# Attention loop: the values' products a round later, six tiles of exponentials

## The chip, the cores and the metric

The kernel runs on one core of a Trainium2 chip. The metric is the device time of one execution in microseconds; the time of a kernel is the median of several runs. The engines are TensorE (PE, with its weight loads listed apart as PEld), VectorE (DVE), ScalarE (ACT), GpSimd (POOL) and SyncE (SP). Each works through its own instructions in the order in which the program has them, and waits for the others by semaphores.

## The reference

Two layers over an image batch of 4 x 64 x 64 x 128 numbers in float32. Layer 0 is a selective scan in three directions. Layer 1 is attention on tokens (16 heads of width 8, where query, key and value are the same vectors), followed by a small dense part, and by experts that pick 8 of 4096 tokens each. What the change touches is the middle of the attention:

```
q = jnp.transpose(qkv, (0, 2, 1, 3))                       # 4 images, 16 heads, 4096 tokens, 8
scores = jnp.einsum('bhsd,bhtd->bhst', q, q) / np.sqrt(D)
attn = jax.nn.softmax(scores, axis=-1)
ctx = jnp.einsum('bhst,bhtd->bhsd', attn, q)
```

## The kernel before, in words

**The attention loop.** `Attention.loop(b, beside)` does this for one image, and runs four times. The 16 heads are taken four at a time (`j`, with the heads 4k + j for k from 0 to 3), the 4096 queries in 8 blocks of 512 (`qb`), the 4096 keys in 32 blocks of 128 (`kc`). A round `i` is one (j, qb, kc), so an image has 4 x 8 x 32 = 1024 rounds and the kernel 4096. The text calls the score products of a round S and the value products V.

- `scores(i)` issues S: four matmuls (L833), one for each of the four heads, each on 32 rows of PE. Two heads share a score tile in PSUM of 2 x 512 columns (`s`, pool `a_ps_s`, three buffers). So a round has a first and a second pair, and two exponentials on ACT (L838), each from a score tile into a tile `e` in SBUF (pool `a_exps`, four buffers). No maximum is subtracted.
- `values(i)` issues V: four matmuls (L847), one for each head, each on 32 columns of PE, that add the exponentials' product with the values to `acc` (pool `a_ps_o`, one buffer). The values carry a column of ones, so that the softmax's denominators are summed along. The sum runs over the 32 rounds of one (j, qb).
- `sums(j, qb, i)` comes after the last of these 32 rounds: ACT copies `acc` to a tile `av` (L856), and the four stores of the heads' results (L862) and the one of the denominators (L865) are put on POOL's queue three rounds later, out of the dictionary `later`. There are 4 x 8 x 4 = 128 such copies.
- `masked(j, qb)` makes the block of queries `qm` in which all but the four heads are zero (DVE, L822), 12 rounds ahead.

The profile records two passes for each of these float32 matmuls, so a round shows eight records of S and eight of V.

**Order.** The loop runs under a manual schedule: each engine gets its instructions in the order in which the code issues them. Before the first round there is `scores(0)`; round i issues `scores(i + 1)`, then `values(i)`, then the copy if a sum has ended, then a mask and stores if they are due, then `beside(i)`. On PE that is S(1), V(0), work beside, S(2), V(1), work beside, and so on; on ACT the two exponentials of round i + 1, the copy, then the beside-work.

**Work beside.** `beside(i)` gives a step to generators that hold the next image's selective scan (exponentials on ACT at L495, scans on DVE at L507, sums over the states on PE at L515, copies of the scan's end values on POOL at L508, stores on POOL from L534 on) and the dense work of the images before and after. In the fourth loop there is no scan left, and little beside-work at all.

[...]

Of the kernel before, what the change touches and what calls it, by code (L numbers as in the profile page):

```python
# [11 lines left out]
F32 = mybir.dt.float32  # L12
# [4 lines left out]
P = 128  # L17
C = 128
L = 4096
NT = L // P  # L20
# [12 lines left out]
QB = 512  # L33
# [570 lines left out]
class Attention:  # L604

    def __init__(self, tc, ctx, loop, w, gate, cols, ident, bank, dram, t1, w_out, sums, sz, x):
        nc = self.nc = tc.nc
        gate_w, gate_b = gate  # L610
# [25 lines left out]
        with tc.tile_pool(name="a_load", bufs=1) as load, tc.tile_pool(  # L636
            name="a_load_ps", bufs=2, space=PSUM
# [36 lines left out]
        nc.gpsimd.memset(self.heads[:, :, :, D], 1.0)  # L674
        self.small = ctx.enter_context(tc.tile_pool(name="a_small", bufs=2))
        self.pieces_of(loop, 2)
        self.big = loop.enter_context(tc.tile_pool(name="a_big", bufs=1))
        self.mid = loop.enter_context(tc.tile_pool(name="a_mid", bufs=2))
        self.exps = loop.enter_context(tc.tile_pool(name="a_exps", bufs=4))
        self.ps_s = loop.enter_context(tc.tile_pool(name="a_ps_s", bufs=3, space=PSUM))  # L680
        self.ps_o = loop.enter_context(tc.tile_pool(name="a_ps_o", bufs=1, space=PSUM))
        self.u, self.q, self.v, self.context, self.total, self.t2 = {}, {}, {}, {}, {}, {}
# [123 lines left out]

    def loop(self, b, beside):

        nc = self.nc
        self.context[b] = self.dram.tile([P, L], F32, name=f"d_ctx_{b}")  # L810
        self.total[b] = self.dram.tile([H, L], F32, name=f"d_sum_{b}")
        qT = self.big.tile([P, L], F32, tag="qT", name=f"qT_{b}")
        v = self.big.tile([P, NT, VPAD], F32, tag="v", name=f"v_{b}")
        for g in range(NT // 4):
            nc.sync.dma_start(out=qT[:, g * 512 : (g + 1) * 512], in_=self.q[b][:, g * 512 : (g + 1) * 512])
            nc.sync.dma_start(out=v[:, g * 4 : g * 4 + 4, :], in_=self.v[b][:, g * 4 : g * 4 + 4, :])
        rounds = [(j, qb, kc) for j in range(4) for qb in range(L // QB) for kc in range(NT)]
        queries, es, accs, later = {}, {}, {}, {}

        def masked(j, qb):  # L820
            t = self.mid.tile([P, QB], F32, tag="qm", name=f"qm_{b}_{j}_{qb}")
            nc.vector.tensor_scalar_mul(t, qT[:, qb * QB : (qb + 1) * QB], self.mask[:, j : j + 1])  # L822
            queries[j, qb] = t

        def scores(i):

            j, qb, kc = rounds[i]
            es[i] = []
            for pair in range(2):
                s_ps = self.ps_s.tile([P, 2, QB], F32, tag="s", name=f"s_{b}_{i}_{pair}")  # L830
                for k in range(2):
                    at = 32 * (2 * pair + k)
                    nc.tensor.matmul(  # L833
                        s_ps[:, k, :], qT[at : at + 32, kc * P : (kc + 1) * P], queries[j, qb][at : at + 32, :],
                        start=True, stop=True,
                    )
                e = self.exps.tile([P, 2, QB], F32, tag="e", name=f"e_{b}_{i}_{pair}")
                nc.scalar.activation(e, s_ps, AF.Exp, scale=1.0 / math.sqrt(D))  # L838
                es[i].append(e)

        def values(i):
            j, qb, kc = rounds[i]
            if kc == 0:
                accs[j, qb] = self.ps_o.tile([P, QB], F32, tag="acc", name=f"acc_{b}_{j}_{qb}")
            for k in range(4):
                h = 4 * k + j
                nc.tensor.matmul(  # L847
                    accs[j, qb][32 * k : 32 * k + 32, :], v[:, kc, h * VW : h * VW + 32],
                    es[i][k // 2][:, k % 2, :], start=(kc == 0), stop=(kc == NT - 1),
                )  # L850
            del es[i]

        def sums(j, qb, i):

            av = self.mid.tile([P, QB], F32, tag="av", name=f"av_{b}_{j}_{qb}")
            nc.scalar.copy(av, accs.pop((j, qb)))  # L856
            cut = slice(qb * QB, (qb + 1) * QB)

            def store():
                for k in range(4):  # L860
                    h = 4 * k + j
                    nc.gpsimd.dma_start(  # L862
                        out=self.context[b][h * D : h * D + D, cut], in_=av[32 * k : 32 * k + D, :]
                    )
                nc.gpsimd.dma_start(  # L865
                    out=self.total[b].rearrange("(k j) t -> j k t", j=4)[j, :, cut], in_=av[D::32, :]
                )

            later[i + 3] = store

        masked(0, 0)
        scores(0)
        for i, (j, qb, kc) in enumerate(rounds):
            if i + 1 < len(rounds):
                scores(i + 1)
            values(i)
            if kc == NT - 1:
                sums(j, qb, i)
            if kc == NT - 12 and i + 12 < len(rounds):
                masked(*rounds[i + 12][:2])  # L880
            if i in later:
                later.pop(i)()
            beside(i)
        for i in sorted(later):
            later[i]()

# [389 lines left out]
def tile_kernel(tc, ctx, x, in_proj_w, dirs, out_proj_w, attn, gate, weight1, weight2, out):  # L1276
# [16 lines left out]
    with ExitStack() as fill:  # L1293
# [7 lines left out]
        with tc.manual_schedule():  # L1301
# [5 lines left out]
            others.rest()  # L1307
    loop = ExitStack()
    block = Attention(tc, ctx, loop, attn, gate, cols, ident, bank, dram, t1, w_out, scans.sums, inputs.sz, x)

    def opening(b):
# [91 lines left out]
```

## Time and profile before

Three runs took 13392.09, 13397.82 and 13401.96 us, the median is 13397.82. The profiled execution took 13404.59 us, the span from its first to its last instruction is 13402.9 us, and PE's mean granted clock was 0.943.

| stretch (us from the start) | what runs | us | per round | PE busy | ACT busy | DVE busy | granted clock |
|---|---|---|---|---|---|---|---|
| 2810.5 to 5371.6 | loop of image 0 | 2561.1 | 2.50 | 2536.7 | 2380.5 | 2091.4 | 0.99 |
| 5371.6 to 7999.5 | loop of image 1 | 2627.9 | 2.57 | 2566.2 | 2382.5 | 2149.1 | 0.99 |
| 7999.5 to 10590.1 | loop of image 2 | 2590.6 | 2.53 | 2544.6 | 2341.9 | 1954.4 | 0.99 |
| 10590.1 to 12952.6 | loop of image 3 | 2362.5 | 2.31 | 2351.8 | 2004.4 | 212.5 | 1.00 |

Busy times are those in which the engine has at least one instruction under way. Matmuls overlap, and the ends that the profile gives for them are modelled; so PE's busy share tells that it is rarely empty, not how fast it goes. For that one compares the starts of successive groups. The table's stretches begin where the first score product of an image starts; between them lie only some microseconds. Before 2810 us lie the inputs and the first image's scan, after 12953 us the last image's dense part and the experts.

For the copies and stores: the copy L856 takes 585 to 727 ns (median 593) and runs 128 times; the stores at L862 take 502 to 606 ns (median 520) to issue, 512 times, and land 1.7 to 8.7 us after that (median 2.2).

### The profile page before, as it was taken

Reading aid. Unit: us, or ns where it says so; the run is one execution under the profiler, and the core shown is the slowest. Engines: PE = TensorE matmul, PEld = TensorE weight load, DVE = VectorE, ACT = ScalarE, POOL = GpSimd, SP = SyncE. Lnnn points to the kernel's source line nnn. Section 1 sums busy time; section 2 is a strip of 40 time slices with the busy share of each in tenths; the row PEclk is TensorE's granted clock in tenths of the full one; section 3 lists DMA queues with packets and bytes.
Section 4 is the critical chain, followed back from the end, with each engine's and each line's share of the span. In section 5 each row is a group of like instructions: output and inputs, shape, how many; then the busy total and the mean of one; then the engine's idle time right before and its main releaser. Section 6 shows DMA issues by size and latency. Waiting matters only on the chain. (4 is left out here: it accounts for less than half of the span.)

```text
span 13402.9 us, 213892 instructions
## 1 busy us (share of the span) xinstructions
PE 12305.7 (92%) x85255; PEld 3948.9 (29%) x85255; DVE 8969.0 (67%) x8565; ACT 10704.2 (80%) x10807; POOL 3464.3 (26%) x4192
## 2 busy tenths in 40 slices
PE   7797978369999999999999999999999999999976
PEld 3232333112222222233332222333323222222224
DVE  6998989678888877888888679888884210000014
ACT  5665656269999998899999889999998888888851
POOL 2333334222333322223333223333331000000001
PEclk8887988679999999999999999999999999999986
DMA  5666666544444444544444545444443100000015
GB/s 143 185 181 178 193 176 194 154 121 120 117 120 113 107 127 120 142 112 116 111 112 112 130 126 130 107 115 114 110 113 98 51 19 9 9 7 30 12 36 178
DMA packets 703778, 1490.44 MB, mean 111 GB/s; under 512 B 185406, under 2 KB 318838, under 8 KB 702774
## 3 DMA queue, kind: packets, MB, share of 16 engines
q1 hardware_dynamic: 512078, 1057.83, 30.6%
q0 software_dynamic: 139584, 300.84, 7.2%
q10 hardware_dynamic: 51112, 118.08, 3.3%
q8 instruction: 667, 10.93, 0.3%
q14 instruction: 337, 2.76, 0.1%
HBM read 1167.22 MB, written 308.94 MB: 110 GB/s over the span
## 5 line engine op out<-in xcount | busy, mean ns | idle before, releaser
L838 ACT ACTIVATE e<-s 128x1024 f32<-128x1024 f32 x8192 | 7905.3, 1027 | 1026.3 <-PE s L833 847.4
L833 PE MATMUL s<-qm,qT 32*128 32x512 f32 x32768 | 5416.6, 642 | 127.9 <-DVE qm L822 76.3
L847 PE MATMUL acc<-e,v 128*32 128x512 f32 x32768 | 4387.5, 607 | 25.1 <-ACT av L856 22.1
L508 POOL COPY ends<-h 128x1 f32<-128x1 f32 x1536 | 1841.9, 1199 | 5104.7 <-DVE h L507 5088.8
L833 PEld LDWEIGHTS s<-qm,qT 32*128 32x128 f32 x32768 | 1790.0, 183 | 3288.8 <-PE s L833 1438.0
L847 PEld LDWEIGHTS acc<-e,v 128*32 128x32 f32 x32768 | 647.0, 108 | 3163.7 <-issue 3027.8
L507 DVE TENSOR_TENSOR_SCAN h<-dA,ends,dB 128x1024 f32<-128x1024 f32 x576 | 1374.5, 2386 | 197.9 <-ACT dA L495 140.9
L507 DVE TENSOR_TENSOR_SCAN h<-delta,ends,du 128x1024 f32<-128x1024 f32 x576 | 1354.1, 2351 | 164.7 <-ACT delta L495 95.5
L495 ACT ACTIVATE dA<-delta,A 128x1024 f32<-128x1024 f32 x768 | 886.8, 1155 | 339.6 <-DMA delta<-d_delta 217.7
L504 DVE TENSOR_TENSOR dB<-du,B 128x1024 f32<-128x1024 f32 x768 | 935.2, 1218 | 211.8 <-PE y L515 193.1
L495 ACT ACTIVATE delta<-delta,A 128x1024 f32<-128x1024 f32 x768 | 886.6, 1154 | 179.4 <-PE y L515 168.8
L509 DVE TENSOR_TENSOR du<-h,C 128x1024 f32<-128x1024 f32 x768 | 940.7, 1225 | 26.3
L509 DVE TENSOR_TENSOR dB<-h,C 128x1024 f32<-128x1024 f32 x768 | 940.7, 1225 | 26.3
L504 DVE TENSOR_TENSOR du<-du,B 128x1024 f32<-128x1024 f32 x768 | 934.2, 1216 | 0.0
L862 POOL DMA_DIRECT2D d_ctx<-av x512 | 262.2, 520 | 1615.9 <-ACT av L856 1609.4
L515 PE MATMUL y<-dB,sel 128*32 128x256 f32 x6144 | 498.1, 397 | 124.3 <-DVE o L531 109.3
L361 PE MATMUL cv<-xn,conv 128*128 128x512 f32 x1024 | 492.4, 640 | 40.7 <-DVE xn L298 18.4
L515 PE MATMUL y<-du,sel 128*32 128x256 f32 x6144 | 494.2, 395 | 25.3 <-DVE du L509 25.3
L507 DVE TENSOR_TENSOR_SCAN h<-dA,dB 128x1024 f32<-128x1024 f32 x192 | 446.9, 2328 | 54.1 <-ACT dA L495 32.1
L507 DVE TENSOR_TENSOR_SCAN h<-delta,du 128x1024 f32<-128x1024 f32 x192 | 440.1, 2292 | 43.1 <-ACT delta L495 18.7
L531 DVE SCALAR_TENSOR_TENSOR o<-us,D,y 128x256 f32<-128x256 f32 x384 | 206.1, 537 | 353.3 <-PE y L515 353.1
L414 PE MATMUL sp<-s,minus 128*128 128x512 f32 x384 | 222.4, 663 | 207.7 <-ACT s L408 207.7
(248 smaller groups left out, 7676.3 us busy)
## 6 DMA issues: line engine op xcount, KB each, us to landing
delta<-d_delta SPq DMA_DIRECT2D x768, 512.0 KB
du<-d_du SPq DMA_DIRECT2D x576, 512.0 KB
du<-d_du ACTq DMA_DIRECT2D x192, 512.0 KB
d_u<-u POOLq DMA_DIRECT2D x48, 1024.0 KB, 5.6
B<-d_bc SPq DMA_DIRECT2D x96, 512.0 KB
C<-d_bc SPq DMA_DIRECT2D x96, 512.0 KB
d_delta<-r POOLq DMA_DIRECT2D x48, 1024.0 KB, 5.4
d_du<-u POOLq DMA_DIRECT2D x48, 1024.0 KB, 6.6
```

The source lines that it names most:

```text
L361: nc.tensor.matmul(ps[:, cut], w["conv"][:, k, m * P : (m + 1) * P], reads(k, g), start=(k == 0), stop=(k == 3))
L414: nc.tensor.matmul(ps[:, cut], sign, t[:, m, cut], start=(i == 0), stop=(i == 2))
L495: nc.scalar.activation(tiles["delta", s], t, AF.Exp, scale=A)
L504: nc.vector.tensor_mul(dB, du, spread[order, c, "B", j % 2])
L507: nc.vector.tensor_tensor_scan(h, dA, dB, first, ALU.mult, ALU.add)
L508: nc.gpsimd.tensor_copy(ends[order, c][:, at : at + 1], h[:, T - 1 :])
L509: nc.vector.tensor_mul(dB, h, spread[order, c, "C", j % 2])
L515: nc.tensor.matmul(y[32 * g : 32 * g + 32, : T // 4], self.sel[:, j // 2, :], hC[:, 256 * g : 256 * g + 256], start=(j == 0), stop=(j == 3),)
L833: nc.tensor.matmul(s_ps[:, k, :], qT[at : at + 32, kc * P : (kc + 1) * P], queries[j, qb][at : at + 32, :], start=True, stop=True,)
L838: nc.scalar.activation(e, s_ps, AF.Exp, scale=1.0 / math.sqrt(D))
L847: nc.tensor.matmul(accs[j, qb][32 * k : 32 * k + 32, :], v[:, kc, h * VW : h * VW + 32], es[i][k // 2][:, k % 2, :], start=(kc == 0), stop ...
L862: nc.gpsimd.dma_start(out=self.context[b][h * D : h * D + D, cut], in_=av[32 * k : 32 * k + D, :])
```

## The change

V is issued a round later. Round i still begins with `scores(i + 1)`, and then issues `values(i - 1)`, not `values(i)`; the last V of an image follows after its last round. The copy and the stores of a finished sum are now called out of `values`, so they come a round later too, the stores still three rounds after their copy. The pool of exponentials grows from four tiles to six, and `av` goes from two tiles to one.

```diff
-        self.exps = loop.enter_context(tc.tile_pool(name="a_exps", bufs=4))
+        self.exps = loop.enter_context(tc.tile_pool(name="a_exps", bufs=6))
@@ values
             del es[i]
+            if kc == NT - 1:
+                sums(j, qb, i)
@@ sums
-            av = self.mid.tile([P, QB], F32, tag="av", name=f"av_{b}_{j}_{qb}")
+            av = self.mid.tile([P, QB], F32, tag="av", bufs=1, name=f"av_{b}_{j}_{qb}")
             nc.scalar.copy(av, accs.pop((j, qb)))
...
-            later[i + 3] = store
+            later[i + 4] = store
@@ the rounds
             if i + 1 < len(rounds):
                 scores(i + 1)
-            values(i)
-            if kc == NT - 1:
-                sums(j, qb, i)
+            if i:
+                values(i - 1)
             if kc == NT - 12 and i + 12 < len(rounds):
                 masked(*rounds[i + 12][:2])
             if i in later:
                 later.pop(i)()
             beside(i)
+        values(len(rounds) - 1)
         for i in sorted(later):
             later[i]()
```

An `e` tile has 2 x 512 float32 numbers in each partition, 4 KB; an `av` tile has 2 KB.

## The prediction

> **What bounds the kernel now.** First I read where the time lies: busy time by stretch puts the four attention loops at 2561, 2628, 2591 and 2363 us of a span of 13402.9, so 76% of it, with PE busy for 98 to 100% of each and ACT for 85 to 93%. The costliest groups on the page come next (busy us, mean ns, idle before and what ended it):
>
> ```profile
> L838 ACT ACTIVATE e<-s 128x1024 f32<-128x1024 f32 x8192 | 7905.3, 1027 | 1026.3 <-PE s L833 847.4
> L833 PE MATMUL s<-qm,qT 32*128 32x512 f32 x32768 | 5416.6, 642 | 127.9 <-DVE qm L822 76.3
> L847 PE MATMUL acc<-e,v 128*32 128x512 f32 x32768 | 4387.5, 607 | 25.1 <-ACT av L856 22.1
> ```
>
> There are 4096 rounds, so 8192 exponentials of 1.03 us, and in each round eight recorded matmuls of scores (S) and eight of values (V), which overlap. ACT waits for scores, 847 us; PE hardly waits for anything that these rows name. As a busy PE is not a PE at its peak, the timeline of a quiet stretch in the last loop, where only S, V and exponentials run, is the third view (start, length, engine, line, count, idle before):
>
> ```profile
> 11500.44 1.07 PE L847 MATMUL acc<-e,v 128*32 128x512 f32 x8
> 11500.60 4.01 ACT L838 ACTIVATE e<-s 128x1024 f32<-128x1024 f32 x4 [0.36 <-PE s L833]
> 11501.44 1.37 PE L833 MATMUL s<-qm,qT 32*128 32x512 f32 x8
> 11502.74 1.07 PE L847 MATMUL acc<-e,v 128*32 128x512 f32 x8
> 11503.73 1.14 PE L833 MATMUL s<-qm,qT 32*128 32x512 f32 x8
> 11504.81 1.07 PE L847 MATMUL acc<-e,v 128*32 128x512 f32 x8
> 11504.97 4.01 ACT L838 ACTIVATE e<-s 128x1024 f32<-128x1024 f32 x4 [0.36 <-PE s L833]
> 11505.80 1.37 PE L833 MATMUL s<-qm,qT 32*128 32x512 f32 x8
> 11507.10 1.07 PE L847 MATMUL acc<-e,v 128*32 128x512 f32 x8
> ```
>
> Starts tell more than lengths here. From V at 11500.44 to V at 11504.81 two rounds take 4.37 us: V 1.00, S 1.30, V 0.99, S 1.08. Without a wait a round would be 1.00 + 1.07 = 2.07, two of them 4.14, so 0.23 us are lost, all inside every second S. The exponentials tell why. The batch from 11504.97 ends its first one at about 11505.99 (1.02 us); S at 11505.80 has begun with its first pair of heads, and its second pair needs a score tile that this exponential reads (there are three score tiles, `a_ps_s`). It starts some 0.24 us late. So a circle sets the pace: first pair of S (1.13 us), exponential (1.02, with 0.15 for handing on), second pair of the next S, then V, then S again: 2.30 + 2.07 = 4.37 us for two rounds.
>
> And what does V wait for? Its last exponential belongs to the batch that ends at 11500.60 + 4.01 = 11504.61; V starts at 11504.81. It is ready 0.20 us early. The waits by line say the same of the whole run (idle us of the line's engine, times):
>
> ```profile
> L847 PE MATMUL acc<-e,v x32768: 592/616/1063, 2815.7 to 12951.4; 128*32 128x512 f32 x200
> ...
>   ACT av L856: 144.8, 207
>   ACT e L838: 12.9, 13
> ...
> ```
>
> ```profile
> L833 PE MATMUL s<-qm,qT x32768: 585/691/1218, 2810.5 to 12948.4; 32*128 32x512 f32 x200
> ...
>   ACT e L838: 278.3, 399
>   DVE qm L822: 133.1, 5
> ```
>
> Waits for exponentials stand at the scores, 278.3 us (399 waits long enough to be listed), and not at the values, 12.9 us. Read instruction by instruction, start against start, the second pairs of S lose 727 us over 2025 of the rounds, and all V but the first of each sum lose 22.5 us: 10.8 before them (26 cases) and 11.7 between their two halves (23 cases).
>
> **The change, part by part.**
>
> *V a round later.* The order on PE becomes S(i+1), V(i-1), work beside, S(i+2), V(i). Nothing is added: 16 records a round, the same durations. V(i)'s wait for the second exponential of round i is taken from it and stands now before S(i+2), whose first pair overwrites the score tile that this exponential read; before, V's wait had covered it. S's second pair keeps its wait for the exponential before. So of the circle above no arrow is gone: V in it counts as 1.00 us of PE, whichever round it belongs to. What can be saved is what V waits, at most 22.5 us. At such a place the exponential is late by a table load or other work on ACT, and the next exponential, which S's second pair needs, ends about 1.0 us after it: before the change V (1.00 us) filled that time, after it S's first pair stands there. PE gets back almost nothing directly; what comes earlier is the first pair's scores for ACT, by 0.2 to 0.3 us. 0.3 x 26 = 8 us is my estimate, between 0 and 22.5.
>
> *The wait that S's first pair gets.* It replaces a wait on PE's own count, one for one. The nearest row is V today: its third matmul carries a wait for ACT, 4096 times, and in the timeline V's eight weight loads lie within 0.16 us, each 0.11 long, so all start within 0.05 us; one by one they start 7 ns apart, the waiting one too. A wait that is already met costs 0, at most 0.05. I take 0, as this is the same kind of wait on the same engine. [...]
>
> *Six tiles of exponentials for four.* With V a round later a tile is held a round longer; two more tiles are just that round. An exponential of round i+1 waited for V(i-1), now for V(i-2): both stand in PE's order right before the S that it waits for anyway. Cost and gain 0. [...]
>
> *The copy of the finished sum (L856, 128 of them, 593 ns).* It moves on ACT behind two more exponentials and what a scan step puts there, together with its V. Queued behind it are the next exponentials, as now. V of the next sum waits for it: 0.25 us each on average, 32 us in all. Slot for slot that wait stays; only which of the beside-work falls next to it changes. Bounds: all 32 us gone, or each of 128 waits for a whole copy, 0.6 us, 77 us, so +45. I take 0.
>
> *One `av` tile for two.* Now a copy waits for the stores of the sum before it. The last store is issued at most 24.0 us after its copy, landing takes at most 8.7 us (row of L862), and the shortest time from copy to copy is 69.1 us. Cost 0; were the cover gone, ACT would stand, up to 128 times.
>
> *The stores (512 + 128 on POOL's queue).* They stay three rounds behind their copy, so a round later against POOL's other work: the `ends` copies and the `d_y` stores behind them. POOL stands at these stores today for 1609 us and nothing in the loop is held by that. DVE's and SP's instructions and their order are the same in both programs. Cost 0.
>
> *The ends of four loops.* One more V after the last S: S 1.07 + V 1.00 + V 1.00 = 3.07 us, while its second exponential ends some 1.2 + 2 x 1.0 = 3.2 us after S began, and the last V waits for that in either order. Cost 0; uncovered, 4 x 1.0 = 4 us.
>
> **Sum.** The profiled execution took 13404.6 us (span 13402.9 and 1.7 around it), 6.8 above the median of 13397.8. 13404.6 - 8 = 13396.6; on the median's scale 13390.
>
> **Rivals.**
> - *Faster: the ready V loosens S's waits after all.* If freeing V lets PE run ahead so that S's second pair no longer meets a running exponential, the listed 278.3 us shrink; half of them gives 13397.8 - 139 = 13259. For it: 847 us of ACT's idle time end with scores. Against it: V stands behind the waiting S in the order, so it can't fill its wait.
> - *Slower: the new wait before S's first pair costs time.* Place: each of 4096 rounds, on PE's path. Price: the upper bound, 0.05 x 4096 = +205, so 13603. It decides from 27 / 4096 = 6.6 ns a round. Against it: the 7 ns steps in V.
> - *Slower by a little: the copies meet worse neighbours,* +45 at most, so 13443; it leaves "no change" when more than 27 of the 45 come.
> - *The change does nothing as ordered.* PE's order does show V shifted by a round; this is no case of its own.
>
> **How the numbers follow.** About 0.2%, 27 us, is what a measurement of this kernel can tell from no change. The forecast, 13390, lies 8 us below the median: chance 0.80, its own range 13370 to 13424. Faster 0.10, the costly wait 0.05, bad neighbours 0.05. The range takes the bounds of V's waits and of the copies on the fast side (22.5 and most of 32, say 25: 13397.8 - 47.5 = 13350), and on the slow side 13425, where bad neighbours begin.
>
> **What would show it.** Right: in the last loop two rounds still take 4.37 us with S at 1.30 and 1.08; V's wait for exponentials gone from 12.9; S's wait for them near 278 or a little above; ACT's wait for scores near 847; copies' wait near 145. Wrong: S no longer split in the quiet stretch (the faster rival), or V-to-S steps grown from 1.00 us (the costly wait).

## The result, and the profile after

The change did nothing that these runs can tell from no change. Four runs of the changed kernel have a median of 13410.91 us (13407.96 to 13417.07), four of the kernel before, taken along, 13399.89 (13392.09 to 13405.19): the ratio is 1.0009, with a 95% interval of 0.9992 to 1.0027. The profiled execution has a span of 13406.4 us, against 13402.9.

The groups of the page after the change answer line by line to those before (busy us, mean ns, idle before and what ended it):

```profile
L839 ACT ACTIVATE e<-s 128x1024 f32<-128x1024 f32 x8192 | 7908.6, 1027 | 1025.7 <-PE s L834 850.9
L834 PE MATMUL s<-qm,qT 32*128 32x512 f32 x32768 | 5423.4, 643 | 126.3 <-DVE qm L823 76.0
L848 PE MATMUL acc<-e,v 128*32 128x512 f32 x32768 | 4386.4, 607 | 24.6 <-ACT av L859 24.3
```

ACT waited 847.4 us for scores and now waits 850.9. The quiet stretch of the last loop has the same beat (timeline of the changed kernel, start and length first):

```profile
11501.82 1.07 PE L848 MATMUL acc<-e,v 128*32 128x512 f32 x8
11501.99 4.00 ACT L839 ACTIVATE e<-s 128x1024 f32<-128x1024 f32 x4 [0.36 <-PE s L834]
11502.82 0.54 PEld L834 LDWEIGHTS s<-qm,qT 32*128 32x128 f32 x8 [0.84 <-issue]
11502.82 1.37 PE L834 MATMUL s<-qm,qT 32*128 32x512 f32 x8
11504.12 1.07 PE L848 MATMUL acc<-e,v 128*32 128x512 f32 x8
11505.12 0.31 PEld L834 LDWEIGHTS s<-qm,qT 32*128 32x128 f32 x8 [0.84 <-ACT e L839]
11505.12 1.14 PE L834 MATMUL s<-qm,qT 32*128 32x512 f32 x8
11506.19 1.07 PE L848 MATMUL acc<-e,v 128*32 128x512 f32 x8
```

From V at 11501.82 to V at 11506.19 two rounds take 4.37 us, and S takes 1.30 in one and 1.07 in the other. Every second S is still split, and ACT still idles 0.36 us per four exponentials. That these V belong to the round before makes no difference to the beat.

One view looks as if much had changed, and it is worth reading with care. These are the waits of the S line, in the changed kernel:

```profile
L834 PE MATMUL s<-qm,qT x32768: 585/692/1218, 2819.0 to 12955.7; 32*128 32x512 f32 x200
...
  issue: 1470.1, 2130
  ACT e L839: 1245.1, 1583
  ACT dA L495: 275.0, 328
  ACT delta L495: 266.6, 318
  DVE qm L823: 133.4, 5
  ACT prob L1085: 3.4, 4
  PE acc L848: 1.4, 1
```

"ACT e" was 278.3 and is 1245.1. But before the change the same list had these lines beside the two shown in the prediction:

```profile
  PE s L833: 1438.0, 1715
  issue: 1426.2, 1972
...
  PE y L515: 114.0, 273
  PE acc L847: 1.3, 1
```

Summed, 1438.0 + 1426.2 + 278.3 + 133.1 + 114.0 + 1.3 gives 3391 us; after the change the seven lines give 3395. Most of it, 2640 us before and 2637 after, is the 0.84 us in which the weight loader (PEld, whose idle time is in this list too) has nothing to do while V streams. The profile puts it down to whatever semaphore the next S names; that was PE's own count and is now ACT's, since the wait moved there. The steps from V's last matmul to the first of an S that follows it directly show that nothing was really waited for: their median is 0.523 us in both kernels, over 3146 and 3144 steps.

### The profile page after: what moved, and what is told of

Same layout as the page of the kernel before. It is cut to its first block, busy times and chain, and to the rows that moved or that the text cites. A ratio compares the mean times of both kernels' runs of the same rounds, so it can differ in the third digit from the quotient of the medians.

```text
span 13406.4 us, 213233 instructions
## 1 busy us (share of the span) xinstructions
PE 12322.0 (92%) x85255; PEld 3953.4 (29%) x85255; DVE 8969.1 (67%) x8565; ACT 10707.2 (80%) x10807; POOL 3468.5 (26%) x4192
## 5 line engine op out<-in xcount | busy, mean ns | idle before, releaser
L839 ACT ACTIVATE e<-s 128x1024 f32<-128x1024 f32 x8192 | 7908.6, 1027 | 1025.7 <-PE s L834 850.9
```

## The experiments

Where the text speaks of a loop's length, it is taken from the start of the image's first score product to the end of its last V, in the profiled execution:

| kernel | first loop starts | image 0 | 1 | 2 | 3 | sum |
|---|---|---|---|---|---|---|
| before | 2810.5 | 2560.7 | 2617.5 | 2580.9 | 2362.0 | 10121.1 |
| before, again | 2809.4 | 2557.7 | 2616.1 | 2580.9 | 2362.1 | 10116.8 |
| changed | 2819.0 | 2558.0 | 2615.9 | 2578.0 | 2369.1 | 10121.0 |
| changed, again | 2820.9 | 2559.6 | 2615.5 | 2580.4 | 2369.1 | 10124.6 |
| six tiles, V in its old place | 2813.9 | 2562.9 | 2617.8 | 2575.3 | 2362.2 | 10118.2 |
| changed, beside-work later too | 2822.6 | 2557.1 | 2610.5 | 2574.4 | 2361.8 | 10103.8 |

The first score products of images 1 and 2 start, in the kernel before, at 5381.4 and 8008.7 us; the stretches of the table of the profile before begin 10 and 9 us ahead of them, where the image before ends.

**Both kernels again.** The kernel before and the changed one, unaltered.

> The kernel before once more, unchanged, to see how far two series and two profiles of one program differ. My theory: ratio 1.000, within 0.1%; the first score product of image 0 starts within some 10 us of 2810.5, and the four loops together take 10121 us give or take 5. Rival (the 11 us between the medians of before and after belong to the change): this one agrees with before within 3 us.

> The changed kernel once more. My theory (the change does nothing): ratio between 0.999 and 1.001, the four loops at 10121 us give or take 5. Rival (a small cost of the change, some 0.1%): again 8 to 14 us above before, and the same loops longer as in the first profile.

The kernel before came to 0.9999 of itself (0.9990 to 1.0008), the changed one to 1.0006 (0.9997 to 1.0015), 9 us at the medians, 13415.70 and 13406.87. By the marks that were set, both rivals have a point: the kernel before agrees with itself within 2 us, and the changed one is again 8 to 14 us above it. A cost of somewhat under 0.1% may well be there, though each interval includes none. In the table one difference comes back to a tenth of a microsecond: the last loop is 7 us longer with the change. The loops as a whole are not. The 8.5 us by which the first loop started later are no sure part of the change: over all kernels run here with the same work up to that point the start lies between 2809 and 2823, and among them one with V in its old place starts at 2820.0 (two score tiles, below) and one with V late at 2811.1 (four tiles).

**The memory part alone.**

```diff
-        self.exps = loop.enter_context(tc.tile_pool(name="a_exps", bufs=4))
+        self.exps = loop.enter_context(tc.tile_pool(name="a_exps", bufs=6))
-            av = self.mid.tile([P, QB], F32, tag="av", name=...)
+            av = self.mid.tile([P, QB], F32, tag="av", bufs=1, name=...)
```

> The memory part of the change alone: six tiles of exponentials and one av tile, V in its old place. My theory: no tile of exponentials is ever short, no copy meets its stores: ratio 0.999 to 1.001, and V's and S's waits as before. Rival one (tiles of exponentials were short): faster, up to half of the 278 us that S waits. Rival two (one av tile makes the copy wait): slower, the copy's line shows waits for the stores.

0.9997 (0.9988 to 1.0006). The S line waits 279.5 us for exponentials, before 278.3; the copy's line shows no wait for its stores. Neither the two tiles more nor the `av` tile less matter by themselves, as far as can be told.

**V late, with four tiles.** The changed kernel with `bufs=4` for `a_exps`.

> V a round later, but with the old four tiles of exponentials. My theory: an exponential of round i+1 then needs the tile that V(i-1) reads, and V(i-1) stands on PE behind S(i+1); the circle becomes V, exponential, second pair of S, V: 1.05 + 1.1 + 1.05 = 3.2 us a round for 2.18 in the quiet loop, and nearly as much in the others, so 16500 to 17500 us. Rival (two more tiles are not needed, the shift alone is the change): 13400.

17007.7 us, 1.268 times before. ACT's exponentials now wait for V, which the list of waits of their line names:

```profile
its engine sat idle before it (us, times) until:
  PE acc L848: 4487.0, 4075
  PE s L834: 22.1, 5
```

4075 of 4096 rounds pay, 1.1 us each, and the loops take 3403 to 3472 us. So the two tiles are the price of the shift: with them it is neutral, without them it costs 27%.

**Two score tiles for three,** in the kernel before and in the changed one.

```diff
-        self.ps_s = loop.enter_context(tc.tile_pool(name="a_ps_s", bufs=3, space=PSUM))
+        self.ps_s = loop.enter_context(tc.tile_pool(name="a_ps_s", bufs=2, space=PSUM))
```

> The kernel before with two score tiles for three, V in its old place. My theory (the score tiles set the pace): the first pair of S then waits for the exponential of the first pair before it, the second pair for that of the second; worked through with 1.13, 1.02 and 0.92 us, rounds of the quiet loop alternate between about 2.3 and 3.0 us, 2.65 on average for 2.18, so 450 us more in the last loop, as much in the others, 14700 to 15300 us in all. Rival (V's wait for exponentials sets the pace): under 13700.

> The changed kernel with two score tiles. My theory: V's place doesn't matter here either, within 30 us of the kernel before with two score tiles. Rival (a V that is always ready gives slack where S waits more): at least 200 us faster than that.

14928.23 us and 14928.41 us, 1.113 times before, with V in the old place and in the new. The quiet stretch of the second shows the two rounds that were worked out, 2.3 and 3.0 us:

```profile
13001.65 1.07 PE L848 MATMUL acc<-e,v 128*32 128x512 f32 x8
13002.64 2.04 PE L834 MATMUL s<-qm,qT 32*128 32x512 f32 x8
13004.62 1.07 PE L848 MATMUL acc<-e,v 128*32 128x512 f32 x8
13005.61 1.38 PE L834 MATMUL s<-qm,qT 32*128 32x512 f32 x8
13006.93 1.07 PE L848 MATMUL acc<-e,v 128*32 128x512 f32 x8
```

V to V is 2.97 us and 2.31 us. One score tile less costs 1519 us, while four tiles of exponentials are as good as six until V is late; and even here, where PE waits much longer at S, a V that is always ready gains nothing. It stands behind the S that waits.

**Exponentials half as long.** Only 256 of a head's 512 queries are exponentiated; the other halves of the tiles hold 1.0. The diff is that of the kernel before; the lines that make these tiles, `self.fixed`, are not shown: there are four of them (six in the changed kernel), set to 1.0 once.

```diff
-                e = self.exps.tile([P, 2, QB], F32, tag="e", name=f"e_{b}_{i}_{pair}")
-                nc.scalar.activation(e, s_ps, AF.Exp, scale=1.0 / math.sqrt(D))
+                e = self.fixed[(2 * i + pair) % 4]
+                nc.scalar.activation(e[:, :, : QB // 2], s_ps[:, :, : QB // 2], AF.Exp, scale=1.0 / math.sqrt(D))
```

> The kernel before, each exponential over 256 of a head's 512 queries, so 512 numbers for 1024 in each partition; the other halves of the four tiles stay 1.0, so the attention's result is not the reference's for them. My theory: an exponential then ends before PE comes back with S, no second pair waits, PE alone sets the pace: the steps of S in a row without beside-work are 2.07 us, and the waits of the second pairs, 778 us in the four loops (235, 206, 189, 148), go: 12550 to 12750 us. Rival (PE busy 98% means that PE is full): 13400, little changed.

> The changed kernel with exponentials over half of the numbers (the same part left out). My theory: within 20 us of the kernel before with half exponentials, as neither has a V that waits. Rival (the new wait before S's first pair costs something once PE is the bound): slower than that one by more than 27 us.

12867.62 us and 12882.37 us, 0.960 and 0.961 times before. The quiet stretch (the first of the two) is PE alone:

```profile
11301.74 1.07 PE L850 MATMUL acc<-e_fixed,v 128*32 128x512 f32 x8
11302.74 1.14 PE L836 MATMUL s<-qm,qT 32*128 32x512 f32 x8
11303.81 1.07 PE L850 MATMUL acc<-e_fixed,v 128*32 128x512 f32 x8
11303.97 1.09 ACT L841 ACTIVATE e_fixed<-s 128x512 f32<-128x512 f32 x2 [0.98 <-PE s L836]
11304.81 1.14 PE L836 MATMUL s<-qm,qT 32*128 32x512 f32 x8
```

V to V is 2.07 us and no S is split. So a PE busy for 98 to 100% of the loops did have 5% to give. I expected 12550 to 12750: of the 778 us lost inside S, counted round by round, 195 stay (37, 73, 51 and 35 us in the four loops), where S is split for other reasons. Of these, 93 us stand in 56 S's during which the granted clock was lowered, which holds stops of PE and slow matmuls behind them; the cause of the other 102 us stays open. The changed kernel is the slower one here by 14.8 us at the medians, 0.1% with two runs each, inside the 27 us that were asked of a costly wait, and on the same side as in the two series with whole exponentials; the steps from V to S are 0.522 and 0.523 us.

**The state sums apart.** An attempt at a faster kernel on this reading: the beside-work on PE in smaller pieces, so that fewer rounds have none. The diff doesn't show `sums` itself, which now takes the number of the one sum to issue.

```diff
             if late:
-                sums(s)
+                sums(s, 0)
                 self.did.add("sum")
             yield
+            if late:
+                sums(s, 1)
+                self.did.add("sum")
             step(s)
```

> The kernel before, with V in its old place; of the scan's state sums (L515) two of a scan step go to PE together now, here the second follows one beside-step later, so that more rounds have some beside-work and fewer have none. My theory: a round without beside-work loses 0.23 us or more to the second pair of S (630 us in the first three loops); 576 more rounds get 0.44 us of work that stands in that time, so up to 0.2 x 576 = 115 us less, 13290 to 13390. Rival one (ACT, busy 91 to 93% there, is the bound in these loops): within 27 us of before. Rival two (the scan waits for its sums): slower.

It is slower by half a per cent, 1.0049 (1.0036 to 1.0062), where I expected up to 115 us less. The second rival was right. DVE, at the end of a scan step, waits for the sums (list of waits of DVE, first the kernel before, then this one; us, times, longest):

```profile
DVE o L531 <- PE y L515: 353.1, 229, 13.3
```

```profile
DVE o L531 <- PE y L515: 870.8, 266, 13.2
```

The time lost inside S did not fall: 780 us for 778 in the four loops. The longer waits stand in the scan: the first loop starts 36 us later, at 2846.6, and the four loops together take 10174.5 us for 10121.1.

**The beside-work a round later too.**

```diff
-            beside(i)
+            if i:
+                beside(i - 1)
         values(len(rounds) - 1)
+        beside(len(rounds) - 1)
```

> The changed kernel with the beside-work called a round later too, so that it stands towards V and the copies as it did before the change and only S is a round ahead of all. My theory (the last loop's 7 us more, 2369.1 for 2362.0, come from the copies, which meet the beside-work of the next round in another place): the last loop takes 2362 give or take 1 again, the whole within 10 us of before. Rival (the 7 us belong to V's delay or to its waits): 2369 stays.

The last loop is back at 2361.8 us (table), and the whole is 0.9994 (0.9985 to 1.0003) of before. So the 7 us come from how the beside-work stands towards V and the copies, and not from V's delay as such. In the last loop a step of beside-work comes every second round, and a sum ends every 32, so the copy always meets the same place of that pattern; shifted by one round against it, most boundaries between sums cost a little more. At the boundary of rounds 577 and 578 the two steps from S to S take 2.40 + 3.16 = 5.56 us before and 2.07 + 3.72 = 5.79 us after the change, 0.23 us more. The timelines show how. In both kernels the first V of the new sum is 0.33 us late for the copy, and eight matmuls of the dense part (`fo`, 1.09 us) stand near it. Before, these two fall into successive rounds, and no S there is split; after, they fall into the same round, and the S before them is split and loses its 0.23 us (it lasts 1.37 us for 1.14). Over the whole last loop the first V's of its sums are late by 7.5 us before, 10.4 after the change, and 7.5 in this version. From the sixth boundary to the twenty-fifth the changed kernel falls behind by 0.22 to 0.34 us at each, 5.1 us in all. Another 1.7 us are lost at one place that is no boundary, round 777: S stops there for a late exponential, and the granted clock then is 0.5 for 6.8 us in both profiles of the changed kernel, and in neither of the kernel before (with six tiles and V in its old place it is so for 3.4 us). So the copies' neighbours are some 5 of the 7 us. This version's four loops sum to 10103.8 us, 17 less than before, 0.13%: not faster by what can be told.

## Why the prediction was right, point by point

- **What bounds the kernel: right, and shown.** The circle of first pair, exponential and next second pair was read off the 4.37 us that two rounds take before, so these don't test it. The tests are the 4.37 after the change, 2.65 forecast on average for two score tiles (2.31 and 2.97, so 2.64), and 2.07 forecast once the exponential is short (2.07). V's wait for exponentials is in none of these.
- **V a round later: right in kind, mis-sized.** I gave it 8 us, out of 22.5 us that V other than the first of a sum "waits". After the change V names no exponential any more, but for the last two of an image, and by the same count these steps still lose 24 us: 12.0 before V and 12.0 between its halves. They sit at the same places, round 964 of the first image before and 963 after. But for one case it was no waiting: before the change all 26 late V's stand where the granted clock was lowered, and so do, but for one, those that lose more than 0.03 us between their halves. That one, in round 777 of image 3, waited 1.2 us for its exponential. The timeline before shows what the others are:

```profile
5213.33 1.94 PE L847 MATMUL acc<-e,v 128*32 128x512 f32 x8
5215.20 1.84 PE L833 MATMUL s<-qm,qT 32*128 32x512 f32 x8
5216.97 1.07 PE L847 MATMUL acc<-e,v 128*32 128x512 f32 x8
```

  V takes 1.94 us for 1.07, and the S behind it 1.77 us to the next V for 1.07: everything on PE is slower there. Ahead of it stands a real stop, but at S: its second pair starts at 5211.33, 3.39 us idle, for an exponential that stands on ACT behind two table loads of 1.28 us (from 5205.64 and 5208.96 on) and the 2.00 us of L759 between them. So the late exponential of the prediction was there, and it held up S, not V. The windows of that stretch and of one at round 605 of image 1 give the granted clock (last but two of the numbers; in the first the slow part ends at 5216.67):

```profile
5214.00:5218.00 4.00, 4.00 (x28) 0.94 (x24) 3.90 (x4) 1.39 (x2) 0.57 (x1) 0.67 0.35 102
6930.00:6936.00 6.00, 6.00 (x26) 0.92 (x24) 5.83 (x5) 3.09 (x4) 2.94 (x4) 0.51 0.63 154
```

  So the step of mine that failed is the reading of late starts as waits without a look at the clock beside them. The real term is 0 within what can be told. V's list of waits for exponentials fell from 12.9 us to 4.0, which is all that there was to save; 9.9 of the 12.9 stand at the last V of each image, the other 3.0 at round 777, and the 4.0 at the last two V's of the images. The same misreading is in the 727 us of the second pairs: 35 of the 2025 split S's have a lowered granted clock during them, and these hold 68 of 782 us (counted from the first to the last matmul of an S).
- **The wait that S's first pair gets: right, 0.** The steps from V's last matmul to S are 0.523 us in both kernels, at the median of 3146 and 3144: with the semaphore already there the new wait adds nothing that these steps show.
- **Six tiles for four: right.** Alone they do nothing (0.9997 times before); with V late they are needed (17007.7 us with four). As far as the runs go, the tiles that count are the scores', where one less costs 1519 us (no run has one more), and not the exponentials' while V stands in its old place.
- **The copies: the bounds held, the value was off.** I took 0 within -32 to +45; it is some +5 of the last loop's +7, and the last loop is back at its old length when the beside-work moves along.
- **One `av` tile, the stores, POOL, the loops' ends: right, nothing seen.** The copy's line lists no wait for its stores.
- **The sum.** -8 + 0 became 0 + 7; the medians of the two series moved by 9 to 11 us, their intervals include no change, and 13410.91 lies in the range, 21 us above the point. Of the 21 us 8 are the V term, and 2 are the median of before, which is 13399.89 over four runs. Another 7 stand in the last loop, though the four loops together are not longer; so where the rest lies is open. The direction of the point was wrong, faster for slightly slower, and the width of the range covered it. That no change can be told was forecast for the right reason: no arrow of the circle went.
- **The rivals.** The faster one fell in the run with two score tiles and V late: 14928 either way. The costly wait fell with the unchanged steps. The neighbours were real, with some 5 us of a possible 45.

## What to carry to other kernels

Before taking a wait off an instruction, look at what that instruction waited: here V was ready 0.2 us before its turn. Follow the circle that sets the beat and see whether the wait is an arrow of it. Look, too, at what stands ahead of the instruction on its engine: in 4092 rounds before the change and 4088 after it no V starts ahead of the S that is issued before it, and with two score tiles, where S waits more, a V that is always ready gained nothing (14928.41 us for 14928.23). And when a wait moves, idle time can change its name in the profile, as "ACT e" went here from 278.3 to 1245.1 us while the line's sum stayed at 3391 and 3395: compare sums of a line's waits, and starts against starts, not one releaser's number.

## What the runs showed of the hardware that was not expected

- PE's granted clock drops to half within the stretch of the loops. In the profile before, 18 stretches of 3.4 to 17.1 us between 5200 and 11000 us have a granted clock of 0.5, and at each of them PE had a stop: 1.8 to 13.7 us from one matmul's start to the next. Of the 30 such steps over 1.5 us in the loops 18 go with a halved clock; the other 12 (1.6 to 3.6 us) do not, so length alone doesn't decide. The 15 V's that lie wholly in the slow stretches take 1.93 to 1.94 us for 1.07, so PE loses time there beside what the stop itself took. The shortest of the 18 steps is 1.8 us, 1.2 us of it idle.
- The kernel is deterministic enough to see 7 us in 13400: the last loop took 2362.0, 2362.1, 2362.2 and 2361.8 us in four profiles with the old phase (the first two of one kernel), and 2369.1 in both profiles with the new one.
